# Two first-layer blocks in one PSUM bank, and later copies and result sums, in a graph layer with a mixture of experts

## The chip, the core and the metric

The kernel runs on one core of a Trainium2 chip. The core has a matrix engine (TensorE, PE in the profile), a vector engine (VectorE, DVE), an activation engine (ScalarE, ACT), a general engine (GpSimd, POOL), and SyncE (SP), which here only issues transfers. Matrix results go to PSUM[...]. The engines run independently, each through its own instructions in order, and wait for each other by semaphores. The metric is the device time of one execution in microseconds (us).

## The reference

6250 nodes with 256 features; 106,250 edges (self loops included), sorted by target. A normalised graph convolution is added to the input, then a feed-forward part with eight experts, two for each node:

```python
deg_isqrt = maximum(segment_sum(ones, dst), 1.0) ** -0.5
x = x + gnn(layernorm(x), deg_isqrt, W, b, src, dst)
x = x + ffn(layernorm(x), Wg, bg, W1, b1, W2, b2)

# gnn:  t = norm * (h @ W.T + b);  return segment_sum(t[src], dst) * norm
# ffn:  scores = x @ Wg.T + bg;  top 2 of 8 experts, softmax over the two
#       out = sum over the two of prob * (relu(x @ W1[e].T + b1[e]) @ W2[e].T + b2[e])
```

## The kernel before

**Stages.** First the degrees are counted with small matmuls and a table of scaled, normalised node rows is written to memory (two fp16 halves for each value). Then comes the chunk loop. The sorted edges are cut into 831 chunks of 128. In the loop, for each chunk s, `gather` (L389) fetches the 128 source rows with one indirect transfer from POOL, six chunks ahead and into 24 buffers; `mask` (L396) makes the 0/1 matrix of targets on DVE, six chunks ahead; `add_up` (L403) multiplies both on PE and adds into a window of 128 nodes in PSUM (`ps`). A node tile has 128 nodes; there are 49.

**What follows a window and a tile.** After the last chunk of a window, `join` adds the window's two halves and the part carried over from the window before on DVE (`rolled`, L478 and L481), and ACT copies the finished nodes into `whole` (L486). From the last chunk of a tile on (`s = FINAL[t] + 1`), a hand-written plan places the tile's work by chunk: `turn_sum` at s + 2 (transposes on PE, L492, and a copy on ACT, L494), `linear` at s + 4 (L501), and from s + 5 on the parts of `route`, one per chunk: layer norm, expert scores, choice of two experts, places in the experts' queues (DVE, small matmuls at L575 and L576, small steps on ACT at L564 and L572), then `sort` (L629 on PE, L630 on ACT) and `send`, eight transfers by SP into the experts' queues in memory (`fhq`, L641).

**Expert steps.** An expert step takes 256 queued rows of one expert (128 in four late steps); there are 56. `fetch` at s + 14 chooses the expert with the most rows, and SP loads its first weights (`w1`, L695), the rows (`xT`, L704) and its second weights (`w2`, L709). From chunk s + 28 on `next_piece` puts one piece of the current step behind each chunk's add-up, at times two: eight calls of `up`, one block of 128 hidden units each, then eight (or four) calls of `down`. A block is two fp32 matmuls over 256 rows (four instructions in the trace, L730) into a `ph` buffer, of which there are two, each in a bank of its own, and a Relu by ACT into `hid` (L732). `down` multiplies `hid` with `w2` into `py` (two buffers, L740); when 128 rows are done DVE adds the bias into `y` (L744), and SP stores it to `fyq` (L746).

**After the loop.** The plan goes on with s counting on: the last tiles, the last seven steps (chosen once s is over `all_sent`), and the read-back of results by POOL (L800), added on DVE (L808) and stored.

What sets the order of work is thus the order in which the program issues it: within a chunk gather, mask, add-up, then the planned tasks (parts of a task in progress first), then the piece. Each engine keeps that order.

Of the kernel before, what the change touches and what calls it, by code (L numbers as in the profile page):

```python
# [19 lines left out]
P = 128  # L20
# [19 lines left out]
FOLLOWS = [t for t in range(FIRST_STEP, NT) for _ in range(1 + (t in EXTRA))]  # L40
USUAL = len(FOLLOWS) + 7
SHORT = 4
W1C = 2 * H + HB
W2C = HB * D + D

# [59 lines left out]
def pieces(n0, n1):  # L105

    parts = []
    while n0 < n1:
        t, p = divmod(n0, P)
        n = min({0: 128, 64: 64}.get(p, 32), n1 - n0)  # L110
        parts.append((t, p, p + n))
        n0 += n
    return parts
# [19 lines left out]
def in_order(ctx: ExitStack, tc: tile.TileContext, g: Shared):  # L133
# [249 lines left out]
    def free_order(ins, others, why):  # L383
        for o in others:
            tc.declare_no_dep(ins.ins, o.ins, reason=why)
# [74 lines left out]
    for j, key in enumerate(sorted(set(kept.values()))):  # L460
        keeps[key] = keep.tile([P, 1], F32, name=f"keep{j}")
        nc.gpsimd.memset(keeps[key], 1.0)  # L462
        for t, p0, p1 in pieces(key[0], key[0] + key[1]):
            nc.gpsimd.memset(keeps[key][p0:p1, :], 0.0)
    whole, turned_sums, turned_inputs = {}, {}, {}

    rolled = None
    placed = known = sent = 0
# [1 line left out]
    def join(w):  # L470

        nonlocal rolled
        n0 = WINDOWS[w][0]
        n1 = WINDOWS[w + 1][0] if w + 1 < len(WINDOWS) else NP
        ps = sums.pop(w)
        new = work.tile([P, D], F32, name="rolled", bufs=3)
        if w:
            nc.vector.scalar_tensor_tensor(new, rolled, keeps[kept[w]], ps[:, 0:D], op0=OP.mult, op1=OP.add)  # L478
        else:
            nc.vector.tensor_copy(new, ps[:, 0:D])  # L480
        nc.vector.tensor_add(new, ps[:, D:2 * D], new)  # L481
        rolled = new
        for t, p0, p1 in pieces(n0, n1):
            if p0 == 0:
                whole[t] = work.tile([P, D], F32, name="whole")
            nc.scalar.activation(whole[t][p0:p1, :], new[p0:p1, :], AF.Copy)  # L486
# [159 lines left out]
    def rows_of(step):  # L646
        return P if USUAL - SHORT <= step < USUAL else FT

# [73 lines left out]
    def up(step, b):  # L722
        f = steps[step]
        w1 = f["w1"]
        n = rows_of(step)
        if b == 0:
            f["hid"] = work.tile([P, HB, FT], F32, name="hid")
        ph = psp.tile([P, FT], F32, name="ph")
        for k in range(2):
            nc.tensor.matmul(ph[:, :n], w1[:, k * H + b * P:k * H + (b + 1) * P], f["xT"][:, :n, k],  # L730
                             start=(k == 0), stop=(k == 1))
        nc.scalar.activation(f["hid"][:, b, :n], ph[:, :n], AF.Relu, bias=w1[:, 2 * H + b:2 * H + b + 1])  # L732

    def down(step, i):
        f = steps[step]
        a = i // 4
        if i % 4 == 0:
            f["py"] = psp.tile([P, D], F32, name="py")
        for b in (2 * (i % 4), 2 * (i % 4) + 1):
            nc.tensor.matmul(f["py"], f["hid"][:, b, a * P:(a + 1) * P], f["w2"][:, b * D:(b + 1) * D],  # L740
                             start=(b == 0), stop=(b == HB - 1))
        if i % 4 == 3:
            y = work.tile([P, D], F32, name="y", bufs=4)
            nc.vector.tensor_add(y, f["py"], f["w2"][:, HB * D:])  # L744
            r0 = P + step * FT + a * P
            w = nc.sync.dma_start(yq[r0:r0 + P, :], y)  # L746
            free_order(w, reads, "results are written once, and read once written")
            writes.append((step, w))
        if i == 4 * rows_of(step) // P - 1:
            del steps[step]  # L750


    tasks = {}

    def plan_at(s, fn, *args):
        tasks.setdefault(s, []).append((fn, args))
# [12 lines left out]

    earliest = {}  # L770
    for t in range(NT):
        s = FINAL[t] + 1
        plan_at(s + 2, turn_sum, t)
        plan_at(s + 4, linear, t)
        in_parts(s + 5, route, t)
        s += LATE[t]
        for i, step in enumerate(k for k, tile in enumerate(FOLLOWS) if tile == t):
            in_parts(s + 14 + 4 * i, fetch, step)
            earliest[step] = s + 28 + 4 * i
    for w, (n0, chunks) in enumerate(WINDOWS):  # L780
        tasks.setdefault(chunks[-1] + 1, []).insert(0, (join, (w,)))
    plan_at(3, centre)
    for t in range(0, NT, 2):
        plan_at(4 + t // 2 * 3, inputs_turned, t, min(t + 2, NT))
        plan_at(6 + t // 2 * 3, inputs_scored, t, min(t + 2, NT))
    plan_at(30, clear_results)
    chosen = loaded1 = loaded2 = len(FOLLOWS)
    all_sent = FINAL[NT - 1] + 1 + 19

    cur = 0  # L790
    done = 0

    def results(t0, t1, bound):

# [24 lines left out]
    def next_piece(s):  # L819

        nonlocal cur, done
        step = done
        if step >= USUAL or "xT" not in steps.get(step, {}) or s < earliest.get(step, 0):
            return
        if cur < HB:
            up(step, cur)
        else:
            down(step, cur - HB)
        cur += 1
        if cur == HB + 4 * rows_of(step) // P:  # L830
            done += 1
            cur = 0

    with tc.manual_schedule():
# [16 lines left out]
        with tc.tile_pool(name="ftail", bufs=2) as pool:  # L851
            s = NC
            pend = []
            plan = list(DONE)
            got = asked = allowed = stored = 0
            latest = 0
            since = {}

            def take():
                nonlocal got, stored  # L860
                t, j, yb = pend.pop(0)[1]
                add_in(t, j, yb)
                got += 1
                if got == 2 * stored + 11:
                    store(stored, stored + 4, nc.gpsimd)
                    stored += 4

            while done < USUAL or tasks or len(plan) > 1 or asked < 2 * allowed or pend:
                for fn, args in tasks.pop(s, []):
                    fn(*args)  # L870
                if s > all_sent:
                    if chosen < min(USUAL, done + 4):
                        run(choose(chosen))
                        chosen += 1
                    if loaded2 < min(loaded1, done + 3):
                        load_second(loaded2)
                        loaded2 += 1
                    if loaded1 < min(chosen, done + (cur >= HB) + 3):
                        load_first(loaded1)
                        load_rows(loaded1)  # L880
                        loaded1 += 1
                was = done
                next_piece(s)
                if done > was:
                    since[was] = s
                if len(plan) > 1 and done > plan[0][0] and s >= since.get(plan[0][0], 0) + 6 \
                        and asked == 2 * allowed:
                    step, t1 = plan.pop(0)
                    results(allowed, t1, float(P + (step + 1) * FT))
                    allowed = t1  # L890
                    latest = step
                if asked < 2 * allowed and s % (4 if s > all_sent else 2):
                    pend.append((s, read_back(pool, rowat, asked // 2, asked % 2, latest)))
                    asked += 1

                if pend and (done == USUAL or len(pend) > 10 or s >= pend[0][0] + 8):
                    take()
                s += 1

            results(allowed, NT, float(P + USUAL * FT))
            late = work.tile([P, NT, 2], F32, name="late", bufs=1)
            missed = work.tile([P, 2], F32, name="missed")
            nc.vector.tensor_tensor(late, at, bounds, op=OP.is_ge)
            nc.vector.tensor_reduce(missed[:, 0:1], late, op=OP.add, axis=mybir.AxisListType.XY)
            nc.vector.tensor_reduce(missed[:, 1:2], most, op=OP.max, axis=mybir.AxisListType.X)
            nc.vector.tensor_scalar(missed[:, 1:2], missed[:, 1:2], float(SLOTS), None, op0=OP.is_gt)
            nc.vector.tensor_add(missed[:, 0:1], missed[:, 0:1], missed[:, 1:2])
            nc.vector.tensor_add(missed[:, 0:1], missed[:, 0:1], g.outside)  # L910
            ones = work.tile([P, 1], F32, name="ones")
            nc.vector.memset(ones, 1.0)
            pm = psp.tile([1, 1], F32, name="pt", bufs=1)
            nc.tensor.matmul(pm, missed[:, 0:1], ones, start=True, stop=True)
            nc.vector.tensor_scalar(g.bad, pm, 1.0, None, op0=OP.min)
            last = [read_back(pool, rowat, t, j) for t in range(allowed, NT) for j in range(2)]
            if stored < allowed:
                store(stored, allowed, nc.sync)
            for t, j, yb in last:
                add_in(t, j, yb)  # L920
                if j:
                    store(t, t + 1, nc.sync if t % 2 else nc.scalar)
# [536 lines left out]
```

## Time and profile before

| | us |
|---|---|
| median of 3 timed runs | 1607.33 (1602.92 to 1615.76) |
| the profiled execution | 1341.47 |
| its span | 1339.7 |
| PE busy | 1179.6 (88%) |
| POOL busy | 903.7 (67%) |
| DVE busy | 985.5 (74%) |
| ACT busy | 402.5 (30%) |
| first gather, last gather, last add-up | 82.0, 1127.3, 1147.9 |

The profiled execution was 266 us shorter than the median of the timed runs. Its mean granted PE clock was 0.956 of full speed. Durations below come from it alone.

In the profile's lines a name such as L730 is the line of the kernel; "ph<-xT,w" is output and inputs. A wait is written as "waiting instruction <- what ended the wait: us in total, times, longest". A bracket at the end of a timeline line is the idle time of that engine just before, and what ended it. The largest groups of PE and ACT work of the change (busy time, mean ns of one | idle time before, and its cause):

```profile
L740 PE MATMUL py<-w,hid 128*128 128x256 f32 x1728 | 435.8, 382 | 3.9 <-DVE y L744 3.9
L732 ACT ACTIVATE hid<-ph,w 128x256 f32<-128x256 f32 (+1 forms) x448 | 204.6, 465 | 291.5 <-PE ph L730 283.8
L486 ACT ACTIVATE whole<-rolled 32x256 f32<-32x256 f32 (+2 forms) x156 | 64.6, 414 | 346.2 <-DVE rolled L481 345.5
```

### The profile page before, as it was taken

What the parts mean: (1) busy time and instruction counts of PE and PEld (TensorE: products, weight loads), DVE (VectorE), ACT (ScalarE), POOL (GpSimd) and SP (SyncE); (2) the same over time, 40 slices, a digit from 0 to 9 for tenths busy, and PEclk for the clock granted to TensorE, in tenths of its full rate; (3) what the DMA queues carried; (4) which work ended last, traced back from release to release, by engine and by line L of the source; (5) the groups of instructions that cost most, each with busy time, mean ns of one, the idle gap of its engine ahead of it and who ended that gap; (6) DMA issues with size and microseconds to landing.
All of it is one profiled execution on the core that took longest, in us unless ns stands there. A gap on an engine that the chain in (4) does not pass through costs nothing.

```text
span 1339.7 us, 23956 instructions
## 1 busy us (share of the span) xinstructions
PE 1179.6 (88%) x6224; PEld 901.0 (67%) x6224; DVE 985.5 (74%) x5327; ACT 402.5 (30%) x931; POOL 903.7 (67%) x984
## 2 busy tenths in 40 slices
PE   4439895999899999999999999999999999889984
PEld 4417562777576677767777676776777777678873
DVE  8842657787888888888888888888877775765542
ACT  2622331232333233332323323233232222222221
POOL 2047777777777777777777777777777775347743
PEclk9999666999999999999999999999999999799987
DMA  8353456788787878788787888877978987679882
GB/s 297 112 160 104 122 138 193 227 282 272 230 250 261 274 239 286 239 268 265 251 289 228 279 258 254 288 240 270 296 229 280 296 305 236 230 235 338 313 314 89
DMA packets 158459, 326.16 MB, mean 243 GB/s; under 512 B 26708, under 2 KB 105256, under 8 KB 143976
## 3 DMA queue, kind: packets, MB, share of 16 engines
q1 hardware_dynamic: 110780, 194.17, 42.1%
q0 software_dynamic: 46864, 129.82, 33.2%
q8 instruction: 51, 0.84, 0.3%
q14 instruction: 96, 0.79, 0.2%
q10 hardware_dynamic: 668, 0.55, 0.1%
HBM read 269.01 MB, written 55.42 MB: 242 GB/s over the span
## 4 chain that ended last, share of the span: by engine, by line
PE 46%; DMA 23%; DVE 16%; issue 5%; SPq 5%; ACT 4%; POOL 2%; POOLq 0%; ACTq 0%; DVEq 0%
PE ph L730 18%; PE py L740 11%; DMA xT<-fhq 8%; PE ps L403 7%; DMA fhq<-ordered 6%; SPq L641 4%; DMA yb<-fyq,rowat 4%; DMA rows<-ftable,src 3%; PE ph L446 2%; PE pt L501 2%; PE px L629 2%; DVE mask L396 2%; DVE y L744 1%; POOL yb L800 1%; DVE rolled L481 1%
## 5 line engine op out<-in xcount | busy, mean ns | idle before, releaser
L389 POOL DMA_INDIRECT rows<-ftable,src x831 | 791.6, 953 | 253.1 <-issue 105.5
L730 PE MATMUL ph<-xT,w 128*128 128x256 f32 (+1 forms) x1792 | 472.4, 392 | 45.4 <-DMA xT<-fhq 35.7
L740 PE MATMUL py<-w,hid 128*128 128x256 f32 x1728 | 435.8, 382 | 3.9 <-DVE y L744 3.9
L730 PEld LDWEIGHTS ph<-xT,w 128*128 128x128 f32 x1792 | 322.5, 192 | 144.8 <-issue 46.6
L740 PEld LDWEIGHTS py<-w,hid 128*128 128x128 f32 x1728 | 329.8, 192 | 80.4 <-DVE y L744 4.1
L403 PE MATMUL ps<-rows,mask 128*128 128x512 f16 x831 | 318.6, 399 | 38.0 <-DMA fyq<-zero 29.9
L732 ACT ACTIVATE hid<-ph,w 128x256 f32<-128x256 f32 (+1 forms) x448 | 204.6, 465 | 291.5 <-PE ph L730 283.8
L396 DVE TENSOR_SCALAR mask<-col_b,rel 128x128 f16<-128x128 bf16 x831 | 210.0, 272 | 28.9 <-PE ps L403 28.8
L486 ACT ACTIVATE whole<-rolled 32x256 f32<-32x256 f32 (+2 forms) x156 | 64.6, 414 | 346.2 <-DVE rolled L481 345.5
L800 POOL DMA_INDIRECT yb<-fyq,rowat x98 | 94.1, 960 | 90.4 <-DVE mx L543 26.2
L403 PEld LDWEIGHTS <-mask 128*128 128x128 f16 x831 | 87.4, 105 | 67.3 <-POOL keep L462 26.1
L744 DVE TENSOR_TENSOR y<-py,w 128x256 f32<-128x256 f32 x108 | 45.4, 421 | 96.2 <-PE py L740 93.3
L478 DVE SCALAR_TENSOR_TENSOR rolled<-rolled,keep,ps 128x256 f32<-128x256 f32 x149 | 70.7, 474 | 18.0 <-PE ps L403 17.6
L808 DVE SCALAR_TENSOR_TENSOR xr<-yb,prob,xr 128x256 f32<-128x256 f32 x98 | 45.7, 482 | 50.7 <-DMA yb<-fyq,rowat 49.6
L481 DVE TENSOR_TENSOR rolled<-ps,rolled 128x256 f32<-128x256 f32 x150 | 63.6, 424 | 5.2
L501 PE MATMUL pt<-gw,uT 128*128 128x264 f32 x196 | 55.9, 411 | 2.0 <-DVE spot L595 2.0
L509 DVE SCALAR_TENSOR_TENSOR xr<-pt,norm,xr 128x256 f32<-128x256 f32 x49 | 23.7, 483 | 41.7 <-PE pt L501 41.5
L446 PEld LDWEIGHTS ph<-wg,turned 128*128 128x128 f32 x196 | 38.6, 289 | 16.8 <-ACT turned L438 16.1
L199 PE MATMUL count<-oh,ol 128*16 128x8 bf16 (+2 forms) x898 | 28.9, 174 | 22.2 <-DVE oh L188 17.9
L501 PEld LDWEIGHTS pt<-gw,uT 128*128 128x128 f32 x196 | 39.4, 203 | 13.5 <-DVE spot L595 2.1
L376 POOL MEMSET zero<- 128x512 f32 x1 | 0.5, 524 | 64.5 <-DMA ftable<-tab 64.5
L199 PEld LDWEIGHTS <-ol 128*16 128x16 bf16 x898 | 28.7, 109 | 22.5 <-DVE ol L185 16.2
(188 smaller groups left out, 1144.6 us busy)
## 6 DMA issues: line engine op xcount, KB each, us to landing
w<-in_W SPq DMA_DIRECT2D x56, 1152.0 KB
w<-in_W SPq DMA_DIRECT2D x56, 1028.0 KB
fhq<-ordered SPq DMA_DIRECT2D x392, 64.0 KB
fyq<-y SPq DMA_DIRECT2D x108, 128.0 KB
xT<-fhq SPq DMA_DIRECT2D x52, 256.0 KB
rows<-ftable,src POOLq DMA_INDIRECT x831
out<-xr POOLq DMA_DIRECT2D x11, 512.0 KB
xr<-in_x SPq DMA_DIRECT2D x6, 896.0 KB
```

What stands on the lines that cost most here:

```text
L389: nc.gpsimd.indirect_dma_start(out=rows[c], out_offset=None, in_=table[:, :], in_offset=bass.IndirectOffsetOnAxis(ap=g.src[:, c:c + 1], ax ...
L396: nc.vector.tensor_scalar(masks[c], g.col_b[:, r:r + P], g.rel[:, c:c + 1], None, op0=OP.is_equal)
L403: nc.tensor.matmul(sums[w], masks.pop(c), rows.pop(c), start=(c == chunks[0]), stop=(c == chunks[-1]))
L446: nc.tensor.matmul(px, xT[:, k, (t - t0) * P:(t - t0 + 1) * P], wg[:, k, :], start=(k == 0), stop=(k == 1))
L478: nc.vector.scalar_tensor_tensor(new, rolled, keeps[kept[w]], ps[:, 0:D], op0=OP.mult, op1=OP.add)
L481: nc.vector.tensor_add(new, ps[:, D:2 * D], new)
L486: nc.scalar.activation(whole[t][p0:p1, :], new[p0:p1, :], AF.Copy)
L501: nc.tensor.matmul(pl, uT[:, k, :], gw[:, k, :], start=(k == 0), stop=(k == 1))
L730: nc.tensor.matmul(ph[:, :n], w1[:, k * H + b * P:k * H + (b + 1) * P], f["xT"][:, :n, k], start=(k == 0), stop=(k == 1))
L732: nc.scalar.activation(f["hid"][:, b, :n], ph[:, :n], AF.Relu, bias=w1[:, 2 * H + b:2 * H + b + 1])
L740: nc.tensor.matmul(f["py"], f["hid"][:, b, a * P:(a + 1) * P], f["w2"][:, b * D:(b + 1) * D], start=(b == 0), stop=(b == HB - 1))
L800: r = nc.gpsimd.indirect_dma_start(out=yb, out_offset=None, in_=yq[0:P + (upto + 1) * FT, :], in_offset=bass.IndirectOffsetOnAxis(ap=where ...
```

## The change

Three things are edited. Two successive blocks of `up` share one `ph` buffer of a whole bank, the even block in its first half and the odd one in its second; the number of buffers stays two. The copies of finished nodes into `whole` become a task of their own, `part_of`, two chunks (`BEHIND`) after the join, and all that is planned from a tile's end moves by two chunks with it, the earliest start of its steps too. The sum and store of a result leave `down` and become a task `leave` of the next chunk; `gone` counts steps whose last result has been stored, and the loads of second weights after the loop go by it. `all_sent` grows by three. Lines below the first edits are one to nineteen higher in the changed kernel.

```diff
+BEHIND = 2
...
         rolled = new
+        summed[w] = new
+
+    def part_of(w):
+
+        n0 = WINDOWS[w][0]
+        n1 = WINDOWS[w + 1][0] if w + 1 < len(WINDOWS) else NP
+        new = summed.pop(w)
         for t, p0, p1 in pieces(n0, n1):
...
-        ph = psp.tile([P, FT], F32, name="ph")
+        if b % 2 == 0:
+            f["ph"] = psp.tile([P, 2, FT], F32, name="ph")
+        ph = f["ph"][:, b % 2]
...
         if i % 4 == 3:
-            y = work.tile([P, D], F32, name="y", bufs=4)
-            nc.vector.tensor_add(y, f["py"], f["w2"][:, HB * D:])
-            r0 = P + step * FT + a * P
-            w = nc.sync.dma_start(yq[r0:r0 + P, :], y)
-            free_order(w, reads, "results are written once, and read once written")
-            writes.append((step, w))
+            plan_at(s + 1, leave, step, a, f["py"], f["w2"])
...
+    def leave(step, a, py, w2):
+
+        nonlocal gone
+        y = work.tile([P, D], F32, name="y", bufs=4)
+        nc.vector.tensor_add(y, py, w2[:, HB * D:])
+        r0 = P + step * FT + a * P
+        w = nc.sync.dma_start(yq[r0:r0 + P, :], y)
+        free_order(w, reads, "results are written once, and read once written")
+        writes.append((step, w))
+        if a == rows_of(step) // P - 1:
+            gone += 1
...
     for t in range(NT):
-        s = FINAL[t] + 1
+        s = FINAL[t] + 1 + BEHIND
...
         tasks.setdefault(chunks[-1] + 1, []).insert(0, (join, (w,)))
+        plan_at(chunks[-1] + 1 + BEHIND, part_of, w)
...
-    all_sent = FINAL[NT - 1] + 1 + 19
+    all_sent = FINAL[NT - 1] + 1 + 20 + BEHIND
...
-                    if loaded2 < min(loaded1, done + 3):
+                    if loaded2 < min(loaded1, gone + 3):
```

More of the change, by code (lines that the diff above doesn't have):

```diff
@@ L464, in in_order @@
             nc.gpsimd.memset(keeps[key][p0:p1, :], 0.0)
-    whole, turned_sums, turned_inputs = {}, {}, {}
+    summed, whole, turned_sums, turned_inputs = {}, {}, {}, {}
     rolled = None
@@ L732, in up, with down @@
         nc.scalar.activation(f["hid"][:, b, :n], ph[:, :n], AF.Relu, bias=w1[:, 2 * H + b:2 * H + b + 1])
-    def down(step, i):
+    def down(step, i, s):
         f = steps[step]
@@ L787, in in_order @@
     chosen = loaded1 = loaded2 = len(FOLLOWS)
-    all_sent = FINAL[NT - 1] + 1 + 19
+    all_sent = FINAL[NT - 1] + 1 + 20 + BEHIND
     cur = 0
-    done = 0
+    done = gone = 0
     def results(t0, t1, bound):
@@ L827, in next_piece @@
         else:
-            down(step, cur - HB)
+            down(step, cur - HB, s)
         cur += 1
```

## The prediction

> **What bounds the kernel now.** I read the page's busy totals first, then busy time by stage, then TensorE's (PE's) waits in the middle stage, then the timeline of single chunks. The stages, in us: start:end length, then busy time (x instructions) of PE, its weight load, DVE, ACT, POOL, then the granted clock, DMA share, GB/s:
>
> ```profile
> 87.00:270.00 183.00, 153.23 (x650) 110.38 (x649) 102.14 (x561) 48.13 (x133) 138.53 (x147) 0.81 0.55 156
> 270.00:1148.00 878.00, 834.90 (x3870) 625.98 (x3870) 711.60 (x4062) 273.94 (x640) 650.17 (x683) 0.99 0.81 261
> 1148.00:1340.00 192.00, 159.62 (x738) 133.36 (x736) 103.50 (x482) 44.88 (x104) 102.95 (x109) 0.90 0.77 263
> ```
>
> The chunk loop's steady part is 270 to 1148. PE is busy 834.9 of 878 us, so all its idle time there is 43 us: that is the most that removing waits can give. The waits behind it (us in total, times, longest):
>
> ```profile
> PE ph L730 <- DMA xT<-fhq: 26.1, 25, 2.8
> PE ph L730 <- ACT hid L732: 8.7, 11, 1.9
> PE ps L403 <- DMA rows<-ftable,src: 5.1, 6, 1.5
> ```
>
> POOL issues a gather every 1.25 us (0.95 busy, 0.30 between), so 831 need 1039 us. It starts at 82 us and issues the last at 1127; PE adds up the last chunk at 1147.9. So two engines run at nearly one pace, and at the end PE is 20.6 us behind the gather it consumes. Time added to PE is not hidden by POOL.
>
> A plain chunk with a first-layer block (start, duration, engine, line):
>
> ```profile
> 602.97 1.07 PE L730 MATMUL ph<-xT,w 128*128 128x256 f32 x4
> ...
> 603.88 0.38 PE L403 MATMUL ps<-rows,mask 128*128 128x512 f16 x1
> ...
> 604.08 0.47 ACT L732 ACTIVATE hid<-ph,w 128x256 f32<-128x256 f32 x1 [0.53 <-PE ph L730]
> 604.10 1.07 PE L730 MATMUL ph<-xT,w 128*128 128x256 f32 x4
> ```
>
> A block is four matmul instructions. PE can issue other work 0.91 us after its start, but its result is complete at 1.07, and its Relu on ACT ends at 604.08 + 0.47 = 604.55, 1.58 after the start. By then the next block has long begun (604.10). How fast PE resumes when it does wait for a Relu, and why Relus come late today:
>
> ```profile
> 337.14 0.84 ACT L486 ACTIVATE whole<-rolled 32x256 f32<-32x256 f32 x2 [6.97 <-DVE rolled L481]
> 338.00 0.47 ACT L732 ACTIVATE hid<-ph,w 128x256 f32<-128x256 f32 x1
> ...
> 338.53 1.17 PE L730 MATMUL ph<-xT,w 128*128 128x256 f32 x4 [1.95 <-ACT hid L732]
> ```
>
> The Relu ends at 338.47, PE starts at 338.53: 0.06 us. ACT's copies of finished sums (L486) wait for DVE's join, and the Relu queues behind them.
>
> **What the Trainium skill says.** "PSUM — Partial Sum Buffer", section "PSUM bank collisions raise a hardware error": two engines must not be in one bank on the same partitions at once, even at different addresses, and compilers order such accesses. The trace before cannot show it, since each block had a bank to itself; but in the changed program as built, every odd block's first matmul waits for the Relu of the even block in its own bank: 224 waits (56 steps x 4). No even block waits for a Relu any more. Before, six blocks of eight waited for the Relu two blocks back. "TensorE: Matmul & The Clock Gate", section "Step-by-step: what each phase is for": matmuls start in program order, only weight loads are pulled ahead, and a stream of matmuls hides each one's drain. The trace agrees: 0.91 us to the next issue against 1.07 to the end. So the new wait exposes drain and Relu, and holds everything behind it on PE. The same page, "Architectural detail": ACT and DVE are strictly in order; the lines at 337 to 338 agree.
>
> **The change part by part.**
>
> 1. Two blocks per bank. The odd block may start 0.06 after the Relu's end, 1.58 + 0.06 = 1.64 us after the even block's start. With one add-up between them (0.22) it would have started at 1.13: it loses 0.51. In the changed order of PE, between even and odd block lie: 122 times only the add-up (0.51 each, 62.2 us); 35 times also the two small counting matmuls of L575/L576 (0.05; 0.46 each, 16.1); 8 times the transposes of L492 (0.22; 0.29 each, 2.3); 5 times the sort of L629 (0.43; 0.08 each, 0.4); 4 times L501's four (0.89; nothing); twice nothing (0.72 each, 1.4). Chunk loop: 82 us.
>
> After the last chunk blocks follow each other directly:
>
> ```profile
> 1184.27 7.38 PE L730 MATMUL ph<-xT,w 128*128 128x256 f32 x32
> 1185.37 0.47 ACT L732 ACTIVATE hid<-ph,w 128x256 f32<-128x256 f32 x1 [4.50 <-PE ph L730]
> 1186.27 0.47 ACT L732 ACTIVATE hid<-ph,w 128x256 f32<-128x256 f32 x1 [0.43 <-PE ph L730]
> ```
>
> A block every 0.90 us; an odd one would start 1.63 after the even one, so loses 0.73. There are 12 such steps, 8 full (31 exposed odd blocks, 22.6 us) and 4 of 128 rows. Those run a block in 0.59, with the Relu starting at 0.70 and taking 0.37: 0.70 + 0.37 + 0.06 - 0.59 = 0.54 each, 16 of them, 8.6 us. Tail: 31 us. Sum 113 us.
>
> 2. Copies of finished nodes two chunks later, with all of a tile's work and the start of its steps. 156 copies, same count and duration. Of the 448 Relus 104 start over 0.1 us late against their block's end, 79 us in all by the instruction records; 50 of these stand behind such a copy on an even block, 41 us. Moved, the copy finds its sum ready and that lateness goes. Without this part those 41 us would be added to the new wait. What stays (11 even Relus behind the copies or exponentials of L494, L564, L572, about 1 us each) costs +9. The 8.7 us of old Relu waits go: -8. Distances between a tile's sort, its eight sends on SP, its xT load and its first block stay 13 chunks; all shift together, as do SP's DMAs. But about two odd blocks of the step before now lie in these chunks, 1.0 us more of PE time, against a mean xT wait of 26.1 / 25 = 1.04: I take -20 (bounds 0 and -26). With PE later, rows are there: -5. First and last step start two chunks later; the loop's end is set by PE's total work, and the same number of first-layer matmuls is left for the tail (second-layer: six more of 166), so that is a shift of order.
>
> 3. Result sums (L744) and their 108 stores (0.33 us each on SP) one chunk later. DVE's 93 us of waiting for py shrink; DVE has 166 us idle in the steady stage, so the gain is none by itself. The store now stands on SP behind the next chunk's sends. A py buffer is held one chunk longer; it is needed again four pieces later, so nothing (bounds -3.9, today's only wait of this kind, and +4 if DVE is stuck on a read-back).
>
> 4. Last seven steps: choosing starts three slots later, one more than the shift, and second weights are gated by stored results. At 0.9 us a piece this is 0 to 6 us; I take 0, as each step lasts 2.1 to 2.9 us longer and gives its loads that room. The waits of the last tiles between 1148 and 1184 (10 us in the trace) get two more pieces as cover: -5.
>
> Sum: 113 + 9 - 8 - 20 - 5 - 5 = **+84 us** on the profiled execution's 1341.5: 1425, or +6.3%.
>
> That execution is far from the median of the three timed runs, 1607.33, and no view shows why. If all stretches are longer, 6.3% gives 1708; if the added waits keep their length, 1607 + 84 = 1691. I forecast **1697 us**.
>
> **The rivals.** (a) The gather pace bounds the timed runs: 266 us more over 831 gathers would be 0.32 us each. Then PE has slack and the loop's 82 us are hidden; the tail's 31 - 5 remain: about 1633. For it: POOL's even beat and PE's waits for rows. Against: in the trace PE ends the loop 20 us behind. (b) Slower PE clock: the 42 us of waits are gone already and nothing is recovered, about 1607 + 113 = 1720. (c) **Faster**: the new wait stays covered and only old waits go. Place: the odd blocks' wait. It decides where the exposed time per odd block falls below 38 / 224 = 0.17 us, 38 being what the terms above recover (8 + 20 + 5 + 5). With none exposed: 1607 - 38 = 1569. Only 10 of 224 odd blocks have that much cover, so this is unlikely. (d) That the wait doesn't exist is excluded by the built order; that the later copies still wait is possible, and adds up to 41: 1738.
>
> **How the numbers follow.** Forecast with (b) and (d) 0.74, (a) 0.17, (c) 0.04, gain and loss cancelling 0.05. About 1% is what a measurement can tell here. Faster 0.04; within 1% 0.06; slower 0.90. The range takes in (a) below and (b) with part of (d) above: 1628 to 1735.
>
> **What would show it.** A wait of PE's first layer for ACT's Relu of about 80 to 120 us, some 200 times, at 0.5 to 0.7 each; copies of whole no longer waiting for DVE; xT and row waits nearly gone; the last add-up at about 1200 instead of 1148, with gathers still 1.25 apart or held up by full buffers. It is wrong if that wait is short, if PE's lateness hides behind POOL, or if the tail, not the loop, carries the difference.

## The result, and the profile after

The changed kernel took 1712.05 us (median of 4 runs, 1707.01 to 1724.36), the kernel before 1611.55 us (4 runs): a ratio of 1.0636, 95% interval 1.0552 to 1.0719. It is slower by about 101 us; 1697 was forecast.

The changed kernel's profiled execution had a span of 1705.2 us, close to its timed runs. The one shown of before (1339.7) is not like its timed runs, so before and after can't be compared from these two. A second profile of the kernel before was taken with the experiments, span 1618.3, and is the one set beside the changed kernel from here on; what separates it from the first is told at the end of the experiments. Busy times of the engines, changed kernel first:

```profile
PE 1286.0 (75%) x6224; PEld 938.2 (55%) x6224; DVE 987.5 (58%) x5327; ACT 403.9 (24%) x931; POOL 902.7 (53%) x984
```

The same line, second profile of before:

```profile
PE 1267.2 (78%) x6224; PEld 939.6 (58%) x6224; DVE 991.1 (61%) x5327; ACT 398.3 (25%) x931; POOL 901.5 (56%) x984
```

The work is the same. PE is busy 19 us more and idle 419 instead of 351 us: of the 87 us between the two spans, 68 are waiting. The groups that answer to those shown of before (busy, mean ns of one | idle before, and its main cause), changed kernel:

```profile
L390 POOL DMA_INDIRECT rows<-ftable,src x831 | 790.5, 951 | 555.9 <-PE ps L404 269.8
L740 PE MATMUL ph<-xT,w 128*128 128x256 f32 (+1 forms) x1792 | 539.3, 430 | 259.6 <-ACT hid L742 197.0
L494 ACT ACTIVATE whole<-rolled 32x256 f32<-32x256 f32 (+2 forms) x156 | 64.0, 411 | 165.9 <-DVE rolled L482 144.2
```

Second profile of before:

```profile
L389 POOL DMA_INDIRECT rows<-ftable,src x831 | 789.0, 949 | 489.5 <-PE ps L403 186.1
L730 PE MATMUL ph<-xT,w 128*128 128x256 f32 (+1 forms) x1792 | 526.1, 425 | 141.0 <-ACT hid L732 66.9
L486 ACT ACTIVATE whole<-rolled 32x256 f32<-32x256 f32 (+2 forms) x156 | 64.5, 413 | 371.8 <-DVE rolled L481 158.8
```

Three readings. First-layer matmuls wait for ACT's Relus 197 us instead of 67. In both, POOL's gathers wait for PE to free row buffers (168 times in the second profile of before, 1.1 us each on average), while PE waits for rows 1 to 2 us in all; so PE, not POOL, sets the loop's pace, and what PE loses there is not hidden by the gathers. And ACT's idle time before the copies, which now stand two chunks later, has fallen from 372 to 166 us; of what is left, 144 us still end with a join of DVE. The last add-up is at 1468.2 us in the changed kernel, 1395.1 before: 73 us come from the loop and 14 from what follows it.

The new wait where nothing covers it, after the loop (timeline of the changed kernel, lines of PE and ACT):

```profile
1558.33 2.08 PE L740 MATMUL ph<-xT,w 128*128 128x256 f32 x8 [0.56 <-ACT hid L742]
1559.54 0.47 ACT L742 ACTIVATE hid<-ph,w 128x256 f32<-128x256 f32 x1 [1.26 <-PE ph L740]
1560.44 0.47 ACT L742 ACTIVATE hid<-ph,w 128x256 f32<-128x256 f32 x1 [0.43 <-PE ph L740]
1560.97 2.08 PE L740 MATMUL ph<-xT,w 128*128 128x256 f32 x8 [0.56 <-ACT hid L742]
```

The PE lines hold an odd block and the next even one: two blocks run through, then PE stands until the even block's Relu (1560.44 + 0.47 = 1560.91) is done, and goes on at 1560.97. A pair takes 2.64 us, against 2 x 0.90 in both profiles of before.

### The profile page after: what moved, and what is told of

It reads as the page before. It is cut to its first block, busy times and chain, and to the rows that moved or that the text cites. A ratio compares the mean times of both kernels' runs of the same rounds, so it can differ in the third digit from the quotient of the medians.

```text
span 1705.2 us, 23939 instructions
## 1 busy us (share of the span) xinstructions
PE 1286.0 (75%) x6224; PEld 938.2 (55%) x6224; DVE 987.5 (58%) x5327; ACT 403.9 (24%) x931; POOL 902.7 (53%) x984
## 4 chain that ended last, share of the span: by engine, by line
PE 56%; DVE 15%; issue 11%; ACT 9%; another core or an unknown queue 6%; DMA 2%; ACTq 0%; POOL 0%; SPq 0%; POOLq 0%; DVEq 0%
PE ph L740 22%; PE py L750 16%; PE ps L404 9%; ACT hid L742 5%; PE pt L509 3%; PE ph L447 2%; DVE mask L397 2%; PE px L637 1%; ACT ordered L638 1%; ACT whole L494 1%; PE px L436 1%; DVE rolled L479 1%; PE count L200 1%; DVE rs L540 1%
## 5 line engine op out<-in xcount | busy, mean ns | idle before, releaser
L740 PE MATMUL ph<-xT,w 128*128 128x256 f32 (+1 forms) x1792 | 539.3, 430 | 259.6 <-ACT hid L742 197.0
L740 PEld LDWEIGHTS ph<-xT,w 128*128 128x128 f32 x1792 | 344.3, 210 | 415.4 <-ACT hid L742 273.2
L404 PE MATMUL ps<-rows,mask 128*128 128x512 f16 x831 | 335.9, 421 | 45.6 <-DMA fyq<-zero 29.7
L742 ACT ACTIVATE hid<-ph,w 128x256 f32<-128x256 f32 (+1 forms) x448 | 208.2, 466 | 557.1 <-PE ph L740 317.0
L404 PEld LDWEIGHTS <-mask 128*128 128x128 f16 x831 | 91.1, 110 | 83.5 <-POOL keep L463 26.1
L494 ACT ACTIVATE whole<-rolled 32x256 f32<-32x256 f32 (+2 forms) x156 | 64.0, 411 | 165.9 <-DVE rolled L482 144.2
L447 PEld LDWEIGHTS ph<-wg,turned 128*128 128x128 f32 x196 | 43.2, 320 | 47.5 <-ACT turned L439 27.1
L447 PE MATMUL ph<-wg,turned 128*128 128x8 f32 x196 | 43.8, 352 | 32.6 <-ACT turned L439 16.7
L638 ACT ACTIVATE ordered<-px 128x512 f32<-128x512 f32 x49 | 30.5, 622 | 107.3 <-remote 44.6
L572 ACT ACTIVATE ex<-ex 128x1 f32<-128x1 f32 x49 | 9.9, 202 | 178.5 <-DVE ex L571 72.5
```

The source lines that it names most:

```text
L404: nc.tensor.matmul(sums[w], masks.pop(c), rows.pop(c), start=(c == chunks[0]), stop=(c == chunks[-1]))
L447: nc.tensor.matmul(px, xT[:, k, (t - t0) * P:(t - t0 + 1) * P], wg[:, k, :], start=(k == 0), stop=(k == 1))
```

## The experiments

Ratios are to the kernel before, timed beside each group of runs on the same chip, with their 95% intervals. The groups stood on four chips, and the kernel before took a different time on each: 1610 us beside the first four runs below, 1589 beside pairs with copies or sums, pairs two apart and copies off ACT, 1615 beside the three runs on three buffers, 1339 beside the last. Differences of a per cent between groups are therefore weaker than those within one. A bank is here what the buffer of a pair takes up, 2 x 256 fp32 values or 2 KB in each partition.

One number is worked out from the start times of all 448 blocks for each profile: the time between the start of an even block and that of the odd one after it, summed over 224 pairs ("into odd blocks"); the same from an odd to the next even block of a step, 168 times ("into even blocks"); and the rest between the first and last block. Each row is one execution, on the chip of its group.

| profile | into odd | into even | rest | first to last block |
|---|---|---|---|---|
| before, first profile (1339.7) | 260 | 229 | 601 | 1091 |
| before, second profile | 337 | 390 | 596 | 1324 |
| changed | 588 | 253 | 568 | 1409 |
| pairs alone | 559 | 259 | 568 | 1386 |
| pairs in half | 471 | 269 | 593 | 1334 |
| later alone | 356 | 376 | 585 | 1317 |
| pairs two apart | 320 | 382 | 588 | 1290 |

**The kernel before again.** Unchanged.

> The kernel before, unchanged, for a second profile: the one shown of before took 1341 us, its timed runs about 1607, and the changed kernel's profile 1705. Theory A (the odd block's wait for the Relu of its own bank) expects, if this profile is of an execution of about 1607 us, the 266 us more to be no added work: busy times as in the first profile within 3%, longer idle time. Theory B (the gathers' issue pace bounds the timed runs) expects gathers about 1.57 us apart because POOL itself is slower, with PE waiting for rows. Theory C (a lower granted PE clock) expects a mean clock near 0.8 and PE busy near 1400 us.

Measured: 1620.06 us (one run), granted clock 0.91. The busy times of DVE, ACT and POOL are within about 1% of the first profile. PE is busy 88 us more, 54 of it in the first-layer matmuls (472.4 to 526.1) and none in the second-layer ones (435.8 and 435.2), and idle 191 us more (351 against 160). Gathers are still 1.25 us apart in the median, but wait for PE: 215 gaps are over 1.4 us, and issues run up to the 24 buffers ahead. Theory B is out. Theory C expected a clock near 0.8 and PE busy near 1400 us; 0.91 and 1267 can make at most a third of the difference. Most of it is waiting.

**The parts alone.** Pairs alone is the `ph` edit in the kernel before; later alone is the changed kernel without it:

```diff
-        ph = psp.tile([P, FT], F32, name="ph")
+        if b % 2 == 0:
+            f["ph"] = psp.tile([P, 2, FT], F32, name="ph")
+        ph = f["ph"][:, b % 2]
```

> Two blocks in one bank alone, copies and result sums where they were. Theory A: the 113 us of odd waits plus the 41 us by which copies of finished sums delay even blocks' Relus, less about 30 us of recovered waits: ratio to before 1.065 to 1.09, at or above the whole change's 1.064. Rival D (the slowdown comes from moving the copies, sums and tile work by one and two chunks, the bank wait being hidden behind the gathers): 1.00 to 1.02.

> The copies two chunks later and the result sums one chunk later, each block in a bank of its own as before. Theory A: 0.97 to 1.00, the old Relu waits and part of the row waits gone. Rival D: 1.05 to 1.07, nearly the whole change.

Pairs alone: 1677.28 us, 1.0429 (1.0371 to 1.0486). Later alone: 1613.46 us, 1.0022 (0.9999 to 1.0045). So the pairs do the harm and rival D falls; but pairs alone cost less than I expected, not more, and with the later parts added the cost rises instead of falling (1.0429 to 1.0636, with 1610 and 1612 us for the kernel before). The table shows how pairs cost: 222 us more into odd blocks, 131 us less into even blocks. Without the pairs, blocks waited two back and Relus could be late; now PE stops at every odd block until ACT has caught up, and even blocks wait for no Relu any more. The price is the difference.

**Half the waits.** Only blocks 0 to 3 of a step are paired:

```diff
-        ph = psp.tile([P, FT], F32, name="ph")
+        if b < 4 and b % 2:
+            ph = f["ph"][:, 1]
+        else:
+            f["ph"] = psp.tile([P, 2, FT], F32, name="ph")
+            ph = f["ph"][:, 0]
```

> Only the first four blocks of a step share banks in pairs (two odd waits in a step in place of four), the last four have a bank each; copies and sums where they were. Theory A: about half of what the run with pairs alone shows over before, 1.03 to 1.05. Rival D: 1.00 to 1.02. If it equals the run with all pairs, the number of waits isn't what counts.

Measured 1629.74 us, 1.0145 (1.0093 to 1.0198): a third of the price, not half. 134 us more into odd blocks, but already 121 us less into even ones: two stops in a step recover nearly as much at the even blocks as four.

**Which later part adds to the pairs.** Both runs are made from the changed kernel. Pairs and copies, with the result sums back in their place:

```diff
-            plan_at(s + 1, leave, step, a, f["py"], f["w2"])
+            leave(step, a, f["py"], f["w2"])
...
-    all_sent = FINAL[NT - 1] + 1 + 20 + BEHIND
+    all_sent = FINAL[NT - 1] + 1 + 19 + BEHIND
```

> Pairs in a bank and the copies (with each tile's work) two chunks later; result sums where they were. Pairs alone gave 1.043, the later parts alone 1.002, both 1.064: 30 us more than the sum. Theory A1 (the moved copies still wait for DVE's joins and now stand before other even Relus): nearly all of the 30 us is here, 1.058 to 1.066. Rival A2 (the later result sums delay DVE's joins, and through them ACT): 1.040 to 1.048 here. The prediction's own step, that moved copies take lateness away from even Relus, would give 1.02 to 1.03.

Pairs and sums, with the copies and the tile work back in theirs:

```diff
-BEHIND = 2
+BEHIND = 0
```

> Pairs in a bank and the result sums one chunk later; copies in the chunk of their join. Theory A1: 1.040 to 1.048, as pairs alone. Rival A2: 1.058 to 1.066.

Pairs and copies: 1676.98 us, 1.0553 (1.0500 to 1.0606). Pairs and sums: 1669.33 us, 1.0476 (1.0391 to 1.0561). Theory A1's band was missed from just below in the first run and met in the second. Set beside the pairs' 1.0429, the copies with their tile work seem to add about 1.2%, but that compares two chips: in us the two runs are alike (1676.98 and 1677.28). Against pairs and sums, on the same chip, the intervals overlap. What is settled is that later copies gave nothing back: the 1.02 to 1.03 of the prediction's step is far outside the interval.

The start times tell why. Take every even block's Relu that starts over 0.1 us after its block's end, count the delay without the 0.04 us of a prompt start, and go back through ACT's instructions as long as they follow each other without a gap of 0.06 us. The first one of this queue, its head, is the one that waited:

| profile | even Relus late, us | head a copy | head `h2s` | head `ordered` | the Relu itself |
|---|---|---|---|---|---|
| pairs alone | 166 | 65 | 24 | 25 | 36 |
| pairs and copies | 170 | 1 | 64 | 47 | 38 |
| changed | 192 | 1 | 51 | 69 | 52 |

Most moved copies do find their sums ready (108 of 156 in the changed kernel), and as heads of a queue that delays an even Relu they are gone. But `h2s` and `ordered`, ACT's other steps of the tile (L572 and L630 in the kernel before), take their place, and the sum does not fall. That moved copies still wait and so hold up other even Relus, as A1 has it, is not what the records show: in the run with pairs and copies 105 us of the delay stand right behind a copy, but only 1 us in a queue that a copy began.

**The same bank, but two apart.** Blocks 0 and 2, 1 and 3 share:

```diff
-        ph = psp.tile([P, FT], F32, name="ph")
+        if b % 4 < 2:
+            f["ph", b % 2] = psp.tile([P, 2, FT], F32, name="ph")
+        ph = f["ph", b % 2][:, b // 2 % 2]
```

> Two blocks in a bank too, but blocks 0 and 2, 1 and 3, and so on share one, so that each block waits for the Relu of two blocks before, as in the kernel before; copies and sums where they were. Theory A (the price is the wait for the Relu of the block just before): 0.995 to 1.005. Rival E (sharing a bank costs by itself, whatever the distance): 1.03 to 1.05, as pairs alone.

Measured 1585.63 us, 0.9984 (0.9960 to 1.0008). Sharing a bank costs nothing that can be measured here; being held to the block just before does. This is the run that decides. The order was kept: no block starts earlier than 0.05 us after the end of the Relu two blocks back, which reads the other half of its bank. PE's waits there (us in total, times, longest):

```profile
PE ph L732 <- issue: 59.8, 42, 3.3
PE ph L732 <- ACT hid L734: 47.6, 25, 3.9
```

With pairs alone, and in the second profile of before:

```profile
PE ph L732 <- ACT hid L734: 163.4, 136, 7.1
PE ph L730 <- ACT hid L732: 66.9, 32, 5.4
```

So 25 waits for Relus, as few as without shared banks. The changed kernel's waits are:

```profile
PE ph L740 <- ACT hid L742: 197.0, 139, 6.4
PE ph L740 <- issue: 39.8, 49, 3.3
...
PE ph L740 <- DMA xT<-fhq: 7.5, 3, 4.6
```

**Copies taken off ACT.** Pairs, with

```diff
-            nc.scalar.activation(whole[t][p0:p1, :], new[p0:p1, :], AF.Copy)
+            nc.vector.tensor_copy(whole[t][p0:p1, :], new[p0:p1, :])
```

> Pairs in a bank, and the 156 copies of finished sums made by DVE right after the join, so that no Relu stands behind a copy that waits for DVE. In the profile with pairs alone even Relus behind such a copy were 94 us late. Theory A: that lateness is part of the price, so the ratio falls from 1.043 to 1.00 to 1.025. Rival F (only the drain and the Relu's own length count, or DVE becomes the bound with some 60 us more work): 1.04 to 1.07.

Measured 1663.01 us, 1.0486 (1.0442 to 1.0530): no gain. With no copies in ACT's queue its heads are others: queues that begin with `h2s` make even Relus 78 us late instead of 24 with pairs alone, and all even Relus together are 147 us late instead of 166. ACT stands at the next wait for DVE instead. My theory of what makes Relus late was right about ACT's queue and wrong that the copies were the cause to remove.

**One block further away.** Three buffers; the bank comes from px and pt sharing one:

```diff
-        ph = psp.tile([P, FT], F32, name="ph")
+        ph = psp.tile([P, FT], F32, name="ph", bufs=3)
...
-        px = psp.tile([P, 2, 2 * P], F32, name="px", bufs=1)
+        px = psp.tile([P, 2, 2 * P], F32, name="pt", bufs=1)
```

(likewise for the other uses of `ph` and `px` ahead of it; the control has the px edits alone, the third run the later parts too).

> The kernel before with three first-layer buffers of a bank each in place of two; the bank comes from giving the tiles px and pt one bank between them. Each block then waits for the Relu three blocks back. Theory A, from the other side (the distance between a block and the Relu it waits for sets the price; 67 us of such waits and 53 us without a named cause stand before first-layer blocks in the second profile of the kernel before): 0.96 to 0.99. Rival H (a wait two back is already free and the loop is bound by PE's work and late handovers): 0.995 to 1.01.

> Control of the run with three buffers: px and pt share one bank, still two first-layer buffers, so one bank lies unused. Both theories: 1.00 to 1.015, the price of the shared bank, which is to be taken off the run with three buffers.

> Three first-layer buffers, with the copies two chunks later and the result sums one chunk later. Theory A: within 0.01 of the run with three buffers alone. If the later parts help only once blocks no longer wait for the Relu two back, it is below it by 0.01 or more.

| waits for the Relu | us | ratio |
|---|---|---|
| three back | 1607.05 | 0.9954 (0.9935 to 0.9974) |
| three back, later parts too | 1602.13 | 0.9941 (0.9912 to 0.9970) |
| two back, px and pt in one bank (control) | 1620.04 | 1.0030 (1.0008 to 1.0052) |

Against the control, the third block of distance gains about 0.8%. Theory A's direction holds, its band (0.96 to 0.99) was too hopeful; rival H's band held the measured 0.9954. PE's waits for Relus fall to

```profile
PE ph L730 <- ACT hid L732: 19.5, 13, 4.2
```

Both runs with three buffers beat the kernel before, by half a per cent. One back, two back, three back: 1.04, 1.00, 0.992 (the last against the control).

**Tile work later, copies at once.** From pairs and copies:

```diff
-        plan_at(chunks[-1] + 1 + BEHIND, part_of, w)
+        tasks[chunks[-1] + 1].insert(1, (part_of, (w,)))
```

> Pairs in a bank and each tile's work (transposes, routing, steps) two chunks later, but the copies of finished sums at once after the join as in the kernel before. Pairs alone gave 1.043, pairs with copies and tile work both later 1.055. Theory A1 (the moved copies stand in front of other even Relus): 1.038 to 1.047. Rival A3 (the later tile work, with its own small steps on ACT, costs the 1.2%): 1.050 to 1.060.

Measured 1446.82 us, 1.0805 (1.0781 to 1.0828), but beside it the kernel before took 1339.38 us (9 runs, 1336.55 to 1344.17), as in the first profile. It can't be set beside the other pair runs, and whether the copies or the tile work cost the 1.2%, if it is real, stays open. It is worth more than that: it prices the pairs under the conditions from which the prediction was worked out. PE's waits:

```profile
PE ph L740 <- ACT hid L742: 121.9, 204, 2.1
...
PE ph L740 <- DMA xT<-fhq: 8.1, 7, 4.8
```

204 waits of 0.60 us, at most 2.1. Into odd blocks 415 us instead of 260, into even blocks 219 instead of 229.

**What separates the two kinds of executions.** The same place in both profiles of before. First profile:

```profile
98.15 1.06 PE L435 MATMUL px<-ident,xr 128*128 128x128 f32 x4
...
99.31 0.60 ACT L438 ACTIVATE turned<-px 128x512 f32<-128x512 f32 x1 [4.17 <-PE px L435]
```

Second profile:

```profile
98.55 1.06 PE L435 MATMUL px<-ident,xr 128*128 128x128 f32 x4
...
113.58 0.60 ACT L438 ACTIVATE turned<-px 128x512 f32<-128x512 f32 x1 [18.05 <-remote]
114.23 1.88 PE L446 MATMUL ph<-wg,turned 128*128 128x8 f32 x8 [13.77 <-issue]
```

PE's transposes end at about 99.2 and 99.6. ACT, which had nothing else to wait for, starts 0.1 us later in the first and 14 us later in the second, where no releaser is named that fits ("remote", "issue"); the semaphore's recorded update is at 113.5. Handovers, from the end of one engine's instruction to the start of the one on another engine that waits for it, are late there, now and then, by microseconds. Over all Relus, the time from the later of "block complete" and "ACT free" to the start sums to 10 us in the first profile, 129 in the second, and 11 in the last experiment. All 14 executions timed with the last experiment, of both kernels, were of the short kind, and they stood on a chip of their own. Whether the chip makes the difference was not tested, and on which chip the first profile was taken is not on record.

## Why the prediction was right, and where not

**The direction and the size** held: 84 us forecast, about 101 measured, +6.4% against +5.6% (1697 to 1607). The mechanism is the forecast one, but part of the size is luck. Between the changed kernel's profile and the second of before, 251 us were added into odd blocks, where the prediction has 122 (113 + 9), and 165 recovered (137 into even blocks, 28 in the rest), where it has 38. The two errors offset each other, and have one source: every term was read from an execution with prompt handovers; in the last experiment, where they were prompt again, 155 us were added and 49 recovered. Of the signs that the prediction named, the last experiment shows the first as written, 204 waits of 0.60 us; the changed kernel has fewer and longer ones, 139 of 1.4 us.

**Step 1, the new wait.** The mechanism is shown: in every profile with all blocks paired, all 224 odd blocks start 0.05 us or more after the even block's Relu, most at 0.05, and pairs two apart cost nothing. The counts of what lies between even and odd blocks are those of the trace. The size, 113 us plus the 9 and the 41 that stay when copies are not moved, is 163; the last experiment, where handovers were prompt and copies not moved, shows 155 more into odd blocks. Its whole sum would be 84 + 41 = 125 us there; 107 were measured. That is near, though the parts differ: even Relus were 49 us late, against 50 in the sum, but only half of it in queues that a copy began, and the rest behind `h2s`. In the changed kernel's own profile the 155 were 251; that late handovers meet the new wait too would fit.

**Step 2, what is recovered**, was too small there. I took 8 us of old Relu waits, from an execution with 8.7 of them. An ordinary execution has 67, and 53 more without a cause; into even blocks 137 us were recovered. The term for xT, -20, held in the last experiment's conditions (35.7 in the first profile's whole span, 8.1 there); in ordinary ones there were 11.2 us to recover, and 7.5 stayed.

**Step 2, the copies**, is the step that failed in the timed executions. I said that moved copies would find their sums ready, that even Relus would be less late by 41 us, and that 9 us behind ACT's other steps of a tile (L494, L564 and `h2s`, L572) would stay; `ordered` (L630) was put at nothing. The first came true for 108 of the 156 copies, and where it counts: of the delay of even Relus, 65 us stood in queues that a copy began with pairs alone, 1 us in the changed kernel. The gain did not follow. With `h2s` or `ordered` at the head of the queue the delay is 120 us in the changed kernel against 49 with pairs alone, all even Relus are 192 us late against 166, and the later parts raised the ratio from 1.0429 to 1.0636. The term of 9 was the one mis-sized: it takes the rest of ACT's queue as prompt. Why the later parts cost, and which of them, is open; and moved copies were never timed with prompt handovers.

**Step 3, result sums**, at nothing: later alone is 1.0022 for both parts together, and the sums' own effect with pairs lies within the intervals.

**Step 4 and the tail**: +26 forecast after the loop, 14 seen; +58 in the loop, 73 seen, each between one pair of profiles. A pair of blocks after the loop takes 2.64 us, where I had 1.80 + 0.73.

**The rivals.** (a) is refuted: gathers wait for PE, in the kernel before as well. (b) is right about the clock, 0.91 and not 0.956, and its 1720 is near, but its reason is not: the old waits were not gone, PE stood idle 351 us before the change. (c) is refuted: the wait was not covered. (d) came true in its effect, as nothing was gained from later copies, though not because they still waited. I saw that the first profile was 266 us short of the median and could not explain it; the terms for stalls of others should have been given a wider band, since all came from that execution.

## What to carry to other kernels

What counted for PSUM here is how many blocks lie between a write and the read it must wait for, not whether blocks share a bank: two halves of one bank used in turn leave no block between, two halves used two apart leave one. The Trainium skill, "PSUM — Partial Sum Buffer", section "PSUM bank collisions raise a hardware error", says that accesses have to be ordered by bank and not by address. The traces agree: no odd block of a pair started before the Relu of the other half had ended. The run with pairs two apart shows that this order costs only where it binds neighbours. Taking one wait out of an engine's queue helps only as far as no other wait stands behind it: copies moved, or taken off ACT altogether, left even Relus nearly as late as they were, or later. And before summing waits from a profile, see whether that execution's time is that of the timed runs: here the stalls of two executions of one kernel differed by 191 us.

## What was unexpected of the hardware

The same kernel took 1339 us beside the last experiment, 1341 in its first profile, and about 1590 to 1615 otherwise, with the same work and a clock of 0.96 and 0.91. The records hold 2029 updates of PE's semaphore in the first profile and 1482 in the second, for 2033 instructions that raise it; the last experiment has 2012 of 2015. That updates are merged when they are delivered late would fit, but was not tested, and what makes them late is open. Also, by the records, four matmuls of a block that start after a wait take 1.17 us, where they take 1.07 in a stream (the prediction's lines at 338.53 and 602.97).
